# A two-layer decoder on one core: layer 1's cross-attention on row halves and column quarters, as a pipeline of single tiles that starts inside the self-attention

## The chip, the cores and the metric

The kernel runs on one core of a Trainium2 chip. The metric is device time in microseconds (us) of one execution. Three runs of the kernel before gave a median of 2326.64 us (2325.31 to 2329.75).

The engines are named as the profile names them: PE (TensorE, matrix multiplies and transposes; PEld is its weight load), DVE (VectorE), ACT (ScalarE), POOL (GpSimd), SP (SyncE, which here only issues DMAs). "PSUM" is the memory that PE writes and that DVE and ACT can read; "SBUF" is the working memory that all engines read.

## The reference: what is computed

Two batches of 1024 tokens with 256 features (2048 tokens in all), and a context of 64 rows for each batch. Two post-norm layers, each of a self-attention, a cross-attention to the context and a feed-forward net, with a layer norm after each of the six. The part that the change rewrites is the fifth of the six, layer 1's cross-attention with 16 heads of 16 features:

```
qh = (x   @ wq.T) split into 16 heads of 16
kh = (ctx @ wk.T) split likewise            # 64 context rows
vh = (ctx @ wv.T) split likewise
z  = qh kh^T / 4                            # per head: 1024 x 64 per batch
z  = where(mask, -1e10, z)                  # mask[b, token, context row]
z  = softmax(z, over the 64 context rows)
z  = (z vh) put back to 256 features
x  = layernorm(x + z @ wo.T)
```

It is followed by a feed-forward net whose inputs are quantised with one scale for the whole tensor: the largest absolute value over all 2048 tokens has to be known before the first matrix product of that net can start. So there is a hard joint between the cross-attention and what follows.

## The kernel before

Tokens are held in 4 groups of 512 (`NG`, `GT`), a group in 4 tiles of 128 tokens (16 tiles, `NT`). The weights and biases of layer 1 are prepared in `prepare`, a generator that the expert feed-forward net of layer 0 (`l0_ffn`) advances by one `yield` per step of its own loop, from step 4 of 32 on, so that this work lies beside the matrix products of that net.

**PSUM and pools.** `bank()` gives one of 3 PSUM banks of 128x512 f32, `wide()` one of 2 pairs of banks (128x1024), `acc()` a single bank of its own. `evac` copies PSUM to SBUF, on DVE and ACT in turn unless `by` names one. `weight` gives one of 5 SBUF buffers.

**What sets the order.** Inside `tc.manual_schedule(engines=...)` the named engines run their instructions in the order in which the Python code issues them; engines that are not named are ordered by the framework's scheduler. Every engine runs its own queue strictly in order; waits between engines are semaphores that the framework puts in.

**Layer 1's self-attention** (`l1_attn`, L1205) is a loop over 128 units, written out by hand for PE, DVE and ACT. A unit does the products of one block of keys (`products`, L1322: 8 matrix products on row halves into two `wide` buffers, then two exponentials of 128x1024 on ACT), the mixing of the block before (`mix`, L1355: 4 products on column quarters into `acc`), and two `maxima` (L1270: 4 products into `bank`s and 4 reductions on DVE) for a step that comes 9 units later. So the last 9 units (119 to 127) have no `maxima`. Everything else is hung onto unit numbers with `at(unit, f, ...)`: projections, stacking DMAs, and for each group of 512 tokens the transposes (`turned`), the residual on POOL, the output product (`output`), the layer norm (`normed`) and the transposed copy of the normed group (`onward`). For group 2 these fall in units 122 to 128; for group 3 they are left for the next stage as `self.ends`.

**Layer 1's cross-attention** (`l1_xattn`, L1647) orders only PE by hand; DVE, ACT and POOL are the scheduler's. It first builds `kblk`, keys laid out as a block diagonal: for each chunk `m` of 8 heads a matrix of 128 rows (8 heads of 16 features) by 512 columns (8 heads of 64 context rows), zero outside a head's own block. Then for each of 16 tiles:

- `queries` (once per group, L1666): 4 products of 128x512.
- `softmax` (L1677): POOL fills a tile with -1e10, PE makes the scores in two products over all 128 rows and 512 columns, DVE copies the unmasked ones over the fill (L1690), DVE takes the maximum per head (L1695), POOL subtracts it (L1696), ACT exponentiates (L1697).
- `turn` (L1700): 8 transposes on PE; ACT copies one half out, DVE the other.
- `mix` (L1716): 8 products with the transposed weights as the stationary side and 34 columns (two heads, each 16 values and a column of ones that gives the sum); DVE takes the reciprocal and scales (L1727, L1729).
- `back` (L1734): 2 transposes; `output` (L1745): 2 products of 256 columns, the residual on DVE, and the layer norm (`normalise`, L165, and `scaled`, L214) for one to three tiles at a time, on DVE. The running maximum for the quantisation goes to `xm`, 9 columns.

PE's program goes through n = 0..18 with `softmax(n + 2)`, `turn(n)`, `output(n - 3)`, `back(n - 2)`, `mix(n - 1)`.

## Time and profile before

| what | value |
|---|---|
| median of three runs | 2326.64 us |
| the profiled execution: its own time | 2326.49 us |
| its span (first to last instruction) | 2324.7 us |
| busy share of the span: PE, PEld, DVE, ACT, POOL | 97%, 67%, 71%, 48%, 39% |
| unit 119 of layer 1's self-attention starts (end of the last `maxima`) | 2093.3 us |
| last mixing product of the self-attention ends | 2122.7 us |
| first scores of the cross-attention start | 2128.4 us |
| last column of `xm` is ready | 2243.0 us |
| rest of the quantised net | to 2324.7 us |
| PE busy from 2122.7 to 2243.0 us | 110.6 of 120.3 us |

The profile's times are counted from the start of the span. A group of instructions is named by its line, its engine and its operation, then output <- inputs by the program's names, with partitions x elements; after it stand the count, the busy time and the mean time of one. PE's records need care: an f32 product shows as two records, and matrix products overlap, so the distance from one start to the next says more than the duration of one.

### The profile page before, as it was taken

To read this page: it belongs to the slowest core of one execution; us is meant where nothing else is said; L and a number is where in the kernel's file an instruction comes from. 1 tells how busy PE (TensorE), PEld (TensorE's weight loads), DVE (VectorE), ACT (ScalarE), POOL (GpSimd) and SP (SyncE) were. 2 spreads that over 40 slices of the span, in tenths; PEclk is the share of its full clock that TensorE was granted. 3 is DMA by queue.
4 is the path that set the end of the run, shared out by engine and by line. 5 is a ranking of instruction groups with operands and counts; after the bars stand their busy time and mean duration, and the time that the engine had idled before them with its cause. 6 is when DMAs were issued, how large, how long until landed. Compare 5 with 4: busy or idle time off the path is not lost.

```text
span 2324.7 us, 37116 instructions
## 1 busy us (share of the span) xinstructions
PE 2253.7 (97%) x13964; PEld 1558.2 (67%) x13969; DVE 1650.6 (71%) x2836; ACT 1117.5 (48%) x1754; POOL 916.0 (39%) x791
## 2 busy tenths in 40 slices
PE   8999999999999999999999999999999999999986
PEld 3555545555546788999999999999744454554752
DVE  5888788998787356555556555456789687994778
ACT  4666566566564322333233333333157565665355
POOL 4676576677566444324334333333211101102420
PEclk9999999999999999999999999999999999999998
DMA  6777678577686120101001011000313121310001
GB/s 155 175 174 170 147 180 185 133 182 176 143 196 165 41 62 1 37 15 31 19 32 37 19 31 37 15 1 1 62 17 51 25 45 28 52 22 1 1 1 37
DMA packets 103831, 168.68 MB, mean 73 GB/s; under 512 B 47602, under 2 KB 65508, under 8 KB 103652
## 3 DMA queue, kind: packets, MB, share of 16 engines
q1 hardware_dynamic: 96804, 147.94, 27.9%
q10 hardware_dynamic: 6848, 18.36, 3.3%
q8 instruction: 111, 1.82, 0.3%
q14 instruction: 68, 0.56, 0.1%
HBM read 34.10 MB, written 2.10 MB: 16 GB/s over the span
## 4 chain that ended last, share of the span: by engine, by line
PE 87%; DVE 6%; ACT 3%; issue 2%; DMA 1%; SPq 1%; POOL 0%; ACTq 0%; DVEq 0%; POOLq 0%
PE unit L1025 17%; PE acc L1073 10%; PE wide L325 10%; PE acc L410 9%; PE bank L1073 7%; PE acc L1362 5%; PE bank L280 4%; PE bank L1285 4%; PE bank L428 2%; PE bank L744 2%; PE wide L1331 2%; PE wide L1338 2%; PE bank L304 2%; DVE most L1295 1%; PE bank L1194 1%
## 5 line engine op out<-in xcount | busy, mean ns | idle before, releaser
L340 DVE TENSOR_REDUCE nm<-wide 128x1 f32<-128x1024 f32 x256 | 300.7, 1214 | 58.2 <-PE wide L325 57.1
L1348 ACT ACTIVATE w<-wide 128x1024 f32<-128x1024 f32 x256 | 248.2, 1021 | 128.4 <-PE wide L1338 127.5
L1295 DVE TENSOR_REDUCE most<-bank 128x1 f32<-128x512 f32 x476 | 295.4, 681 | 16.1 <-PE bank L1285 15.5
L325 PE MATMUL wide<-k,q 64*128 64x512 f32 x1024 | 264.3, 624 | 9.3 <-ACT p L345 7.6
L356 POOL TENSOR_SCALAR p<-p,sums 128x1024 f32<-128x1024 f32 x128 | 143.4, 1121 | 249.2 <-DVE sums L353 249.2
L410 PE MATMUL acc<-turned,v 128*64 128x256 f32 x2048 | 235.1, 382 | 0.2 <-issue 0.2
L410 PEld LDWEIGHTS acc<-turned,v 128*64 128x64 f32 x2048 | 141.8, 137 | 111.5 <-issue 35.0
L1014 ACT ACTIVATE mhT<-mhT,cols 128x256 f32<-128x256 f32 (+1 forms) x256 | 143.4, 607 | 146.5 <-DVE mhT L1042 103.4
L345 ACT ACTIVATE p<-wide,nm 128x1024 f32<-128x1024 f32 x128 | 142.8, 1115 | 125.0 <-DVE nm L340 104.6
L923 POOL TENSOR_TENSOR hs<-hs,mhT 128x1024 f32<-128x1024 f32 x31 | 102.4, 3304 | 237.5 <-DVE hs L921 220.2
L1025 PE MATMUL unit<-xT,w 128*128 128x256 f32 x768 | 182.2, 379 | 0.0
L370 DVE STREAM_TRANSPOSE blocks<-p 128x1024 f32<-128x1024 f32 x128 | 158.0, 1234 | 25.3 <-DMA turned<-blocks 9.2
L1082 DVE SCALAR_TENSOR_TENSOR r<-acc,gates,r 128x128 f32<-128x128 f32 x256 | 77.7, 345 | 138.1 <-PE acc L1073 138.1
L325 PEld LDWEIGHTS wide<-k,q 64*128 64x128 f32 x1024 | 89.8, 186 | 126.2 <-issue 78.1
L370 DVE STREAM_TRANSPOSE blocks<-r 128x1024 f32<-128x1024 f32 x128 | 153.8, 1202 | 0.0
L1025 PEld LDWEIGHTS unit<-xT,w 128*128 128x128 f32 x768 | 140.9, 190 | 17.0 <-issue 0.5
L356 POOL TENSOR_SCALAR r<-r,sums 128x1024 f32<-128x1024 f32 x128 | 143.8, 1124 | 0.0
L345 ACT ACTIVATE r<-wide,nm 128x1024 f32<-128x1024 f32 x128 | 142.1, 1111 | 0.0
L1285 PE MATMUL bank<-kst,qst 64*128 64x512 f32 x476 | 133.1, 471 | 9.2 <-DVE most L1295 8.0
L1362 PE MATMUL acc<-w,v 128*32 128x512 f32 x1024 | 137.6, 606 | 1.1 <-ACT w L1348 1.1
L1285 PEld LDWEIGHTS bank<-kst,qst 64*128 64x128 f32 x476 | 66.8, 185 | 107.0 <-DVE most L1295 80.9
L393 POOL COPY turned<-blocks 32x1024 f32<-32x1024 f32 x128 | 131.9, 1031 | 4.0 <-DVE blocks L370 0.3
(351 smaller groups left out, 4373.7 us busy)
## 6 DMA issues: line engine op xcount, KB each, us to landing
turned<-blocks SPq DMA_DIRECT2D x636, 128.0 KB, 2.4
turned<-blocks ACTq DMA_DIRECT2D x132, 128.0 KB, 2.5
w<-in_L_ffn_W SPq DMA_DIRECT2D x16, 1024.0 KB, 5.5
q<-q SPq DMA_DIRECT2D x64, 128.0 KB, 2.4
k<-k SPq DMA_DIRECT2D x32, 128.0 KB, 2.3
qst<-qh SPq DMA_DIRECT2D x48, 64.0 KB
qst<-ql SPq DMA_DIRECT2D x48, 64.0 KB, 2.3
kst<-kh SPq DMA_DIRECT2D x48, 64.0 KB, 2.3
```

The lines of the kernel that those rows point to most:

```text
L325: nc.tensor.matmul(sc[h][:, kb, :], lhsT=q[rows, qi, at : at + P], rhs=k[rows, ki, :], start=True, stop=True,)
L340: nc.vector.tensor_reduce(nm, sc, AX.XY, ALU.max, negate=True)
L345: nc.scalar.activation(p, sc.rearrange("p a c -> p (a c)"), AF.Exp, bias=nm, accum_out=sums[:, 0, h : h + 1],)
L356: nc.gpsimd.tensor_scalar(p, p, sums[:, 1, h : h + 1], 1.0, ALU.mult, ALU.mult)
L370: nc.vector.transpose(blocks[m][:, :, :, h, qt, :], p.rearrange("p (k r q) -> p r k q", r=4, q=32))
L410: nc.tensor.matmul(av[own[h], 0:256].rearrange("p (t i q) -> p i t q", t=2, i=4), lhsT=vals[u][:, kt, own[h]], rhs=p[:, h], start=kt == 0, ...
L1025: nc.tensor.matmul(v[:, m, :], lhsT=up[e][k][:, f : f + P], rhs=self.halves[g][k], start=k in (1, 2, 5) and m == 0, stop=True, skip_group_ ...
L1073: nc.tensor.matmul(ps[at][:, m * P : (m + 1) * P], lhsT=h[k][:, c, m * P : (m + 1) * P], rhs=down[e][k][:, c, :], start=k in (1, 2, 5) and ...
L1285: nc.tensor.matmul(sc[a], lhsT=stack[b, jp, "q"][rows, q0 : q0 + P], rhs=stack[b, jp, "k"][rows, kb * 512 : (kb + 1) * 512], start=True, s ...
L1295: nc.vector.tensor_reduce(most[n][:, kb, qt, h : h + 1], sc[a], AX.X, ALU.max, negate=True)
L1348: nc.scalar.activation(slot[:, k, :], ps[k].rearrange("p a q -> p (a q)"), AF.Exp, scale=0.25)
L1362: nc.tensor.matmul(mixed[n][o : o + 32, :], lhsT=vals[b][:, kt, 17 * h : 17 * h + 32], rhs=pT[:, a, :], start=kt == 0, stop=kt == 7, tile_ ...
```

## The change

Eight things are done.

1. **Scores on row halves.** The 128 rows of a chunk are split into two halves of 64 rows (4 heads each); each half needs only the 256 columns of its own heads. Instead of 2 products of 128 rows x 512 columns there are 4 of 64 rows x 256 columns, two at a time on the two halves of the array.
2. **The mask as a product.** `prepare` transposes the mask (`masked`, bf16) and builds `never` (-1e30 on a diagonal, bf16). Two bf16 products on row halves put the mask into PSUM first; the scores are added to it. The fill on POOL, `keep` and the predicated copy go. In `prepare` this adds four steps, each one DVE copy, four bf16 transposes and one copy out of PSUM, and four `yield`s, so all that follows in the generator comes four steps later.
3. **Sums and division before the mixing.** The column of ones goes. DVE sums the exponentials (`weights`), takes the reciprocal, and POOL multiplies the tile by it. So a tile now has two POOL passes of 128x1024 (subtract, multiply) and, for the last two tiles, each pass is split between POOL and DVE.
4. **Mixing on column quarters.** The values become the stationary side (32 columns), two transposed tiles the moving side (256 columns): 8 products per two tiles. The result is already transposed, so `back` goes.
5. **Who copies.** ACT copies the raw scores out (`copied`), and both halves of the transposed tile, the mixed result and the layer norm's scaling are ACT's; DVE keeps the maximum (now read from PSUM), the sum, the residual and the statistics.
6. **One tile per step, all engines by hand.** The loop over u = 4..21 orders PE, DVE, ACT and POOL.
7. **Four tiles inside the self-attention.** `keys` (the block-diagonal keys, now on POOL) at unit 84, the queries of group 0 at units 118 and 119, the scores and copies of tiles 0 to 3 at units 120, 122, 124, 126, their exponentials and divisions at 123, 125, 127 and in the next stage. These copies go through two `bank`s each and are on DVE.
8. **POOL by hand in the self-attention.** POOL joins the engines that run in program order there.

The layer norm works on two tiles at a time, and `xm` has 8 columns. The diff, cut to its core:

```diff
@@ l1_attn
+            self.l1_cross()
+            x = self.cross
+            at(last - 44, x["keys"])
+            for m in range(2):
+                at(last - 10 + m, x["queries"], 0, m)
+            for n in range(4):
+                for f in ("scores", "copied"):
+                    at(last - 8 + 2 * n, x[f], n)
+                for f in ("exponentials", "weights") if n < 3 else ():
+                    at(last - 5 + 2 * n, x[f], n)
...
-            engines = {mybir.EngineType.PE, mybir.EngineType.DVE, mybir.EngineType.Activation}
+            engines = {
+                mybir.EngineType.PE, mybir.EngineType.DVE, mybir.EngineType.Activation,
+                mybir.EngineType.Pool,
+            }
@@ prepare
-        nc.vector.tensor_scalar(self.keep, mask, 0.0, None, ALU.is_equal)
...
+        for n in range(0, T // P, 4):
+            both = tmp.tile([P, 4, 2, SK], BF16, tag="both", name="both")
+            nc.vector.tensor_copy(both, mask[:, n : n + 4, :].unsqueeze(2).to_broadcast([P, 4, 2, SK]))
+            ps = self.ps_t.tile([P, 1024], BF16, tag="t", name="bankb")
+            for i in range(4):
+                nc.tensor.transpose(
+                    ps[:, i * P : (i + 1) * P], both[:, i].rearrange("p a k -> p (a k)"), self.identb
+                )
+            self.evac(self.masked[:, n * P : (n + 4) * P], ps[:, 0 : 4 * P])
+            yield
@@ new: l1_cross
+        def queries(g, m):
...
+            self.evac(qT[g][:, m, :], ps, 0.25, by=nc.scalar if m and g else nc.vector)
+        def scores(n):
...
+            if n < 4:
+                ps = [self.bank() for _ in range(2)]
+            else:
+                both = self.wide()
+                ps = [both[:, a, :] for a in range(2)]
+            raw[n] = ps if n < 4 else both
+            for r, a in zip(rows, range(2)):
+                nc.tensor.matmul(
+                    ps[a], lhsT=self.masked[r, n * P : (n + 1) * P],
+                    rhs=self.never[r].rearrange("p h k -> p (h k)"), start=True, stop=True,
+                    skip_group_check=True,
+                )
+            for m in range(2):
+                for r, a in zip(rows, range(2)):
+                    nc.tensor.matmul(
+                        ps[a][:, m * 256 : (m + 1) * 256], lhsT=qT[g][r, m, i * P : (i + 1) * P],
+                        rhs=self.kblk[r, g // 2, m, 4 * a : 4 * a + 4, :].rearrange("p h k -> p (h k)"),
+                        start=False, stop=True, skip_group_check=True,
+                    )
+        def scaled(n, by, op):
+            p = prob[n]
+            halves = [(nc.gpsimd, 0, H)]
+            if n >= NT - 2:
+                halves = [(nc.gpsimd, 0, H // 2), (nc.vector, H // 2, H)]
...
+        def copied(n):
...
+            if n < 4:
+                for a in range(2):
+                    nc.vector.tensor_copy(
+                        p[:, 8 * a : 8 * a + 8, :].rearrange("p h k -> p (h k)"), ps[a]
+                    )
+                nc.vector.tensor_reduce(nm, p, AX.X, ALU.max, negate=True)
+            else:
+                src = ps.rearrange("p a (h k) -> p (a h) k", k=SK)
+                nc.scalar.copy(p, src)
+                nc.vector.tensor_reduce(nm, src, AX.X, ALU.max, negate=True)
+            scaled(n, nm, ALU.add)
+        def exponentials(n):
+            if n < NT:
+                nc.scalar.activation(prob[n], prob[n], AF.Exp)
+        def weights(n):
...
+            nc.vector.tensor_reduce(z, prob[n], AX.X, ALU.add)
...
+            nc.vector.reciprocal(rz, z)
+            scaled(n, rz, ALU.mult)
@@ l1_xattn
+            def mix(r):
...
+                ps = self.acc().rearrange("p (c q) -> p c q", c=2)
                 for c in range(2):
+                    for q in range(4):
+                        o = slice(32 * q, 32 * q + 32)
+                        nc.tensor.matmul(
+                            ps[o, c, :], lhsT=self.vblk[:, r // 4, 4 * c + q].rearrange("p a i -> p (a i)"),
+                            rhs=turned[r][:, 4 * (q // 2) + 2 * c + q % 2, :], start=True, stop=True,
+                            tile_position=(0, 32 * q),
+                        )
...
+                self.evac(mixed[r], ps, by=nc.scalar)
             def output(n):
...
                 nc.vector.tensor_tensor(res[g][:, i, :], ps, self.x[g][:, i, :], ALU.add)
+                if k:
+                    moments[r] = self.moments(res[g], range(i - 1, i + 1))
+            def normed(r):
...
+                by = nc.vector if r == NT // 2 - 1 else nc.scalar
+                self.scaled(new[g], res[g], range(i, i + 2), *moments.pop(r), by)
...
+                for m in range(2):
+                    x["queries"](1, m)
+                turn(0)
+                for u in range(4, NT + 6):
+                    turn(u - 3)
+                    x["scores"](u)
+                    x["exponentials"](u - 1)
+                    x["copied"](u)
+                    x["weights"](u - 1)
+                    output(u - 5)
+                    if u % 2:
+                        normed((u - 7) // 2)
+                        x["queries"]((u + 4) // 4, u // 2 % 2)
+                    else:
+                        mix((u - 4) // 2)
+                    if u < 8:
+                        self.ends[u - 4]()
```

## The prediction

> **What bounds the kernel now.** I read the page first, then busy time by stretch, the cross-attention's groups, the chain of waits, and the order in time. On the page PE is busy 97% of the span; by stretch this holds from the end of the last `maxima` (2093.3 us) to the last column of `xm` (2243.0).
>
> ```profile
> core 0: us, PE busy (x) PEld busy (x) DVE busy (x) ACT busy (x) POOL busy (x), PEclk, DMA share, GB/s
> 2093.30:2122.70 29.40, 27.96 (x189) 12.09 (x186) 8.61 (x22) 20.54 (x25) 5.22 (x8) 1.00 0.01 2
> 2122.70:2243.00 120.30, 110.58 (x620) 80.41 (x620) 88.72 (x183) 39.25 (x61) 48.94 (x42) 0.99 0.00 1
> ```
>
> In the self-attention's tail (first row) DVE and POOL are mostly free, ACT is not. In the cross-attention PE binds: tile 1's `turn` starts at 2145.74, tile 14's at 2223.94, so a tile takes 6.0 us. The groups, kept apart by shape:
>
> ```profile
> L1686 PE MATMUL wide<-w,lxqT 128*128 128x512 f32 x64 | 30.9, 606 | 0.0
> L1696 POOL TENSOR_TENSOR lxp<-lxp,lxnm 128x1024 f32<-128x1024 f32 x16 | 30.4, 1902 | 34.0 <-DVE lxnm L1695 34.0
> L1722 PE MATMUL acc<-vblk,lxpT 128*128 128x34 f32 x256 | 29.9, 273 | 0.0
> L1695 DVE TENSOR_REDUCE lxnm<-lxp 128x16 f32<-128x1024 f32 x16 | 19.3, 1209 | 0.0
> L1697 ACT ACTIVATE lxp<-lxp 128x1024 f32<-128x1024 f32 x16 | 16.9, 1058 | 21.8 <-POOL lxp L1696 21.8
> ```
>
> POOL, DVE and ACT wait here for each other (34.0, 21.8) under PE's cover. The chain of waits shows the same three once, where PE does not cover them, before the first tile (start, us, what):
>
> ```profile
> 2130.52 1.31 DVE lxp L1690
> 2131.86 1.23 DVE lxnm L1695
> 2133.16 1.91 POOL lxp L1696
> 2135.09 1.06 ACT lxp L1697
> ```
>
> A hop between engines costs 0.02 to 0.08. The end of the tail in time: ACT's layer norm of group 2 stands ahead of the last exponentials, and PE waits 1.14 for them.
>
> ```profile
> 2117.69 2.07 ACT L224 ACTIVATE xg<-r,off,rstd 128x256 f32<-128x256 f32 x4
> 2119.66 1.92 ACT L1348 ACTIVATE w<-wide 128x1024 f32<-128x1024 f32 x2
> 2120.72 1.96 PE L1362 MATMUL acc<-w,v 128*32 128x512 f32 x8 [1.14 <-ACT w L1348]
> ```
>
> **The change part by part.** *PE.* A tile costs 6.2 now: scores 1.72 (L1686), `turn` 0.87, mixing 1.71 (L1722), `back` 0.22, output 0.86, queries 0.86. Scores on f32 row halves have a row in layer 0 (L325, 8 records of 512 columns in 1.92): 8 records of 256 take 0.96; the mask pair 0.23 (a pair in L1331); together 1.2. Column quarters (L1362) take 1.0 per 8 records of 512; two tiles' mixing has 16 of 256, 1.0, so 0.5 a tile. New sum: 1.2 + 0.87 + 0.5 + 0.86 + 0.86 = 4.3.
>
> *The loop.* PE's 4.3 doesn't set the pace; the order does. In the built program the maximum's only wait is ACT's copy of the same tile. Copying 1024 columns from PSUM I price as L1348, 1.02; the maximum from PSUM as L1290, 1.21. With u's copy ending at 0, in an even unit: maximum to 1.24, POOL's subtraction (1.90) 1.32 to 3.22, exponential to 4.31, next copy to 5.23 (back-to-back instructions overlap by about 0.1 on ACT, 0.07 on DVE). In an odd unit the layer norm of two tiles sits on ACT between copy and exponential, and its offset stands on DVE behind maximum 1.24, sum 2.38, reciprocal 2.60, residual 2.95, offset 3.04. ACT then scales twice (0.59, 0.49) to 4.15, copies two halves to 5.11, exponentiates to 6.07, copies to 6.99. Two units take 12.2, so 6.1 a tile: PE's 6.0 again, now on a chain over ACT, DVE and POOL. The queries' ACT copy adds 0.5 in unit 11. Units 8 to 14: 37.1; 14 to 15, with the subtraction split, 5.0.
>
> *The tail.* Unit 121's mixing ends at 2103.8 now. Add 3.5 (two query units of 1.75), 0.5 (tile 0's scores, 1.2, less 0.7 of a wait they fill), 1.2 (tile 1's): 2109.0, called s. Unit 122's transposes end at s+1.4 (one bank is awaited), unit 123 at 5.4, 124 at 10.9, 125 at 13.0, unit 126's mixing at 15.2, tile 3's scores at 16.4. DVE copies (1.3) and reduces (1.21) them before it reaches group 2's offset, s+19.1; ACT, which waits for it with the last exponentials behind, scales to 21.2 and exponentiates to 23.0; the last mixing ends at s+23.6 = 2132.6, against 2122.7 now: +9.9. Bounds: +6.5 (8.3 of added PE work less the 1.8 of waits) and +14 (DVE's sums queued ahead as well); I keep the walk's value. The keys (4 POOL passes at unit 84, at most 1.27 each, L922) hide in POOL's 0.58 of 20 us.
>
> *Filling.* Transposed group 1.1, wait for `raw` 0.65, quotient 0.55, queries 3.45, two `turn`s 1.8, scores 1.2, 0.25 of waits, then 1.3 on ACT: the first loop copy (unit 4) ends at 2142.9. Units 4 to 8 also carry group 3's end. Unit 4 takes the even 5.2. In unit 5 PE has queries (1.75) and two output products (3.45) ahead of the next transposes and scores, and POOL a residual of 2.38 (L1410) ahead of its subtraction: 7.9. In unit 6 DVE reaches group 3's offset 4.5 after the copy; ACT then scales four times (2.07), copies two halves (0.96), exponentiates (0.96) and copies (0.92): 9.4. Unit 7 has offset 3.04, scaling 1.1, queries 0.5, a transposed copy 0.5, halves, exponential and copy 2.84: 8.0. In all 30.5; between 24 (four units at 6.1) and 35 (if unit 5's two delays add up).
>
> *Draining.* After unit 15's copy: DVE is 0.6 late with the maximum, split passes collide on two SBUF inputs (L923, below: about 1.6 instead of 0.95, four times), the last exponential ends at 9.3 behind an offset (6.3), two scalings and two copies; then sum 10.6, reciprocal 10.8, split product 12.4. DVE's half of the last copy comes after the statistics of tiles 10 and 11 and the maximum of the pair before: 17.2. Mixing 1.0, copy 0.6, output 0.5, then DVE still has an offset and a maximum before it (22.1); residual 0.4, statistics 1.3, power 0.8, scaling 0.9, maximum 0.7, with 0.3 of hops: 26.5 (20 without this queueing, 30 if every half collides in full).
>
> Sum: 2142.9 + 30.5 + 37.1 + 5.0 + 26.5 = 2242.0, against 2243.0: -1.0. To it come three small terms. PE is idle 3.6 us at the end of the tail; the trace has a gap like it:
>
> ```profile
> 1694.28 0.66 PE L1316 MATMUL bank<-ident,cz 128*128 128x128 f32 x4 [3.27 <-POOL cz L1309]
> 1690.00:1695.00 5.00, 1.59 (x10) 1.00 0.57 93
> 1695.00:1700.00 5.00, 4.61 (x20) 0.54 0.01 3
> 1700.00:1705.00 5.00, 5.00 (x36) 0.78 0.00 0
> ```
>
> (the last three: granted clock third from the right). After 3.27 idle it fell to 0.54 and 0.78, some 3.4 us of PE time; I take +1.5 (0 to 3.4), as PE waits for ACT in part of it. The Trainium skill (TensorE: Matmul & The Clock Gate, Part 1) says that one idle window of about 3.4 us halves the clock and a busy one restores it; by it alone this term would be 1.7. `prepare`: 16 bf16 transposes at 0.09 (L1605, 36 in 3.0) beside a PE that is full, and the steps that move towards the end: +2 (0 to 4; its DVE copies, at most 0.7 each, hide under PE, with DVE busy 13.8 of 20 us there, and cost that much each if they don't; SP's loads of these weights move with them, behind two loads of experts' weights; PE waits for no load of this stage in the trace). POOL in program order in the self-attention: +1 (0 to 2: at worst something waits once for the 2.0 memset at L1236). Together +4.5, less the 1.0: +3.5. The profiled execution took 2326.5 (0.15 under the median), so 2330.
>
> The skill's rule that speaks against the change: tiling speeds up TensorE but not the emptying of PSUM, which may become the bottleneck (TensorEngine Tiling (Array Packing), PSUM Bottleneck). By it, counting ACT's copies, exponential and layer norm as throughput, 4.1 a tile, PE would still bind and the time be 2305; the chain above, from this trace's rows, is slower than either throughput.
>
> **The rivals.**
> *The shared SBUF side* (slower). Two-input DVE passes of layer 0 stretch POOL's:
>
> ```profile
> L923 POOL TENSOR_TENSOR hs<-hs,mhT x31: 2351/3333/3398, 871.8 to 1622.7; 128x1024 f32<-128x1024 f32 x31
> L1696 POOL TENSOR_TENSOR lxp<-lxp,lxnm x16: 1900/1902/1905, 2133.2 to 2223.6; 128x1024 f32<-128x1024 f32 x16
> ```
>
> (minimum/median/maximum ns.) If the sums, which now run beside POOL, do this too, 1.90 becomes 2.85: +0.95 in each of 11 units, 2340. Against it: 16 passes at L1696 kept within 5 ns beside DVE's one-input work. It decides from 2.3 a pass on.
> *The layer norm doesn't delay ACT* (faster): if offsets are ready when ACT's copy ends, scaling fits in POOL's 1.9 and units 6, 7, 9, 11, 13, 15 save 3.4, 3.0, 1.8, 2.2, 1.8, 1 (their lengths less the even 5.2, as far as the offset alone makes them): 2317. Against it: DVE's built order.
> *PE stays the bound* (faster): 4.4 a tile, 11 units in 48 instead of 72.6: 2305. For it only PE's present 97%.
> *Halves don't run side by side* (the change doesn't do what it says): scores cost 2.0, +4 in tail and filling, 2334. Against it: L325.
>
> **How the numbers follow.** What a measurement here can tell from no change is about 0.2%, 4.7 us. The walk holds with 0.55 (2323 to 2337: 0.36 within 0.2%, 0.18 above, 0.01 below); SBUF side 0.15; no delay 0.15; PE bound 0.07; halves 0.08 (0.06 slower, 0.02 the same). So faster 0.23, same 0.38, slower 0.39. The range 2315 to 2343 leaves out 2305 and the rest of the tails.
>
> **What would show it.** Right: the last mixing of the self-attention near 2133, copies from PSUM at alternating distances of about 5.2 and 7.0, ACT's layer norm waiting for DVE, POOL at 1.9, the drain 25 or more. Wrong: equal distances below 5.5 (PE or no delay), POOL over 2.3, a tail that grows by less than 6, or a granted clock under 0.9 through the loop.

## The result, and the profile after

The changed kernel takes 2339.89 us (median of four executions, 2338.3 to 2342.1) against 2325.97 of the kernel before beside it (2322.45 to 2329.75): a ratio of 1.006, 95% interval 1.0042 to 1.0078. On a second occasion, at the end of the experiments, the same two took 2341.19 and 2330.95: 1.004 (1.0025 to 1.0055). So it is slower by about half a per cent, more than the 0.2% that can be told from no change. Predicted were 2330 and a range of 2315 to 2343, with 0.38 for "within 0.2%" and 0.39 for "slower": the time lies in the range, some 10 us above the point. As a change, +3.5 us were predicted and 13.9 came.

The profiled execution after took 2339.48 us, its span 2337.7, so 13.0 longer than before's 2324.7. To find where, I cut both spans at seven events that both traces have, and took the differences of their times:

| stage, from the event of the row above to | before, us | after, us | difference | predicted |
|---|---|---|---|---|
| the first `unit` matmul on the experts (L1025 on `xT`, `w`) | 836.3 | 836.3 | 0 | 0 |
| the last such matmul starts | 799.9 | 805.8 | +5.9 | +2 |
| DVE's first early maximum starts | 31.3 | 34.1 | +2.8 | 0 |
| its last early maximum starts | 24.8 | 24.8 | 0 | 0 |
| the last maximum starts (end of the self-attention's steady part) | 400.7 | 401.8 | +1.1 | +1 |
| the last self-attention mixing ends (the tail) | 29.8 | 40.8 | +11.0 | +9.9 |
| the last column of `xm` starts (cross-attention) | 119.9 | 110.7 | -9.2 | -10.9, +1.5 for the clock |
| the end of the span | 82.1 | 83.4 | +1.3 | 0 |

(Each is rounded to 0.1; unrounded, the rows add to 13.0.) The trade that the prediction is mostly about, a longer tail for a shorter cross-attention, came out at +1.8 where +0.5 was predicted. The time was lost ahead of it: 8.7 us before the first maximum of layer 1, in a part of the kernel that the change hardly seems to touch.

Busy time by stretch after; these are the tail and the cross-attention, the two stretches that the prediction showed of before:

```profile
core 0: us, PE busy (x) PEld busy (x) DVE busy (x) ACT busy (x) POOL busy (x), PEclk, DMA share, GB/s
2103.50:2143.60 40.10, 36.12 (x233) 16.65 (x232) 21.05 (x36) 23.20 (x27) 15.32 (x11) 0.98 0.00 1
2143.60:2255.00 111.40, 83.32 (x508) 52.95 (x508) 71.80 (x140) 57.96 (x90) 56.56 (x40) 0.88 0.00 1
```

PE was busy for 110.6 of 120.3 us in the cross-attention, now for 83.3 of 111.4: it no longer binds. No other engine does either; DVE, the next, has 64%. What binds is an order of short waits. The groups, by shape, of tail and cross-attention (busy us, mean ns of one, then the idle time ahead of them):

```profile
L1767 DVE TENSOR_REDUCE lxnm<-wide 128x16 f32<-128x1024 f32 x12 | 14.7, 1224 | 23.8 <-ACT lxp L1766 9.1 <-ACT kh L1766 6.3 <-ACT ql L1766 4.9
L1731 PE MATMUL wide<-v,lxqT 64*128 64x256 f32 x96 | 13.8, 407 | 3.2 <-ACT lxqT L76 3.2
L1825 PE MATMUL acc<-lxpT,vblk 128*32 128x256 f32 x128 | 11.3, 428 | 3.4 <-DVE lxqT L72 1.8 <-ACT lxpT L74 1.3 <-DVE lxpT L70 0.2
L1743 POOL TENSOR_TENSOR lxp<-lxp,lxnm 128x1024 f32<-128x1024 f32 x4 | 7.6, 1903 | 13.8 <-DVE lxnm L1767 13.8
L1724 PE MATMUL wide<-never,masked 64*128 64x512 bf16 x24 | 4.9, 405 | 0.0
```

Row halves and column quarters do what they say: the scores of twelve tiles (L1731) take 13.8 us and the mixing of all sixteen (L1825) 11.3, where before each took some 30 for sixteen. POOL's pass keeps its 1.90. DVE's maximum waits for ACT's copy of the same tile, POOL for the maximum. The chain of waits shows one odd unit and one even unit whole (start, us, what):

```profile
2203.91 0.91 ACT lxp L1766
2204.84 1.23 DVE lxnm L1767
2206.07 1.14 DVE lxz L1778
2207.23 0.25 DVE lxrz L1780
2207.48 0.28 DVE r L1846
2207.76 0.38 DVE off L219
2208.17 1.09 ACT xg L224 x2
2209.26 0.48 ACT lxqT L76
2209.74 0.96 ACT lxpT L74 x2
2210.70 0.96 ACT lxp L1772
2211.66 0.91 ACT qh L1766
2212.59 1.24 DVE lxnm L1767
2213.96 1.91 POOL qh L1743
2215.89 1.06 ACT qh L1772
2216.95 0.91 ACT ql L1766
```

The lower four steps are the even unit that was predicted (maximum, subtraction, exponential, copy), the upper ones the odd unit, with the offset `off` as the fifth thing that DVE does after ACT's copy. Where the 8.7 us arise is shown by two other views. In the experts' stretch, PE's waits after and before:

```profile
PE bankb L1560 <- DVE both L1557: 4.1, 4, 1.0
```

```profile
PE bank L1572 <- DVE twice L1566: 1.1, 1, 1.1
```

(us in all, times, longest). L1560 are the four transposing steps that the change puts into `prepare`. In order of time, the first of them:

```profile
989.70 0.61 DVE L1082 SCALAR_TENSOR_TENSOR r<-acc,gates,r 128x128 f32<-128x128 f32 x2 [0.48 <-PE acc L1073]
990.22 0.41 DVE L1557 CAST both<-mask 128x512 bf16<-128x512 uint8 x1
990.69 0.40 PE L1560 MATMUL bankb<-identb,both 128*128 128x128 bf16 x4 [1.03 <-DVE both L1557]
```

The cast needs nothing of this moment (the mask was loaded long before), but it stands in DVE's queue behind an expert's sum, which itself waits for the matmuls just done. PE, whose next work are the transposes, stands still for the sum and the cast, 1.04 us, four times over. And ahead of the first maximum, the order of time at PE and at the queues that load the stacks:

```profile
1668.68 2.05 PE L1073 MATMUL acc<-w2s,mhT 128*128 128x128 f32 x16 [0.70 <-DVE r L1082]
1670.57 1.95 PE L1073 MATMUL bank<-w,hs 128*128 128x128 f32 x16
1670.76 0.51 SPq L1263 DMA_DIRECT2D qst<-xg  x1
1670.77 0.52 ACTq L1263 DMA_DIRECT2D qst<-xg  x1
...
1675.22 1.17 PE L1287 MATMUL wide<-kst,qst 64*128 64x512 f32 x4 [2.70 <-DMA qst<-xT]
```

The first stacks of the queries leave at 1670.76, as a matmul of the last expert ends, and PE then waits 2.70 us for them. SP's queue waited for this matmul:

```profile
SPq L1263 <- PE acc L1073: 5.4, 1, 5.4
```

The same wait in the kernel before:

```profile
SPq L1261 <- DVE r L1082: 6.3, 2, 5.9
```

There it was a DVE result that the queue waited for (5.9 us at the longest), and the first of these loads left 10.1 us after the first projection (L1194) began, not 18.7. A load that waits for a matmul which has nothing to do with its data waits for memory. In the built programs, the tiles of `qst` lay at bytes 142816 to 159200 of a partition before; the change opens the pools `qk` and `lxq` ahead of `la1` and `st`, so that they now lie at 181984 to 198368, over the experts' `mhT` (171104 to 187488) and `hs` (192608 to 204896), which the last experts' matmuls read to the end. (Before, the two upper ones of the four tiles lay over the other buffer of `mhT`, but the tile that is filled first did not.)

### The profile page after: what moved, and what is told of

Its sections match the earlier page's. It is cut to its first block, busy times and chain, and to the rows that moved or that the text cites. A ratio compares the mean times of both kernels' runs of the same rounds, so it can differ in the third digit from the quotient of the medians.

```text
span 2337.7 us, 36999 instructions
## 1 busy us (share of the span) xinstructions
PE 2239.8 (96%) x13916; PEld 1538.6 (66%) x13921; DVE 1648.3 (71%) x2813; ACT 1140.2 (49%) x1787; POOL 932.7 (40%) x792
## 4 chain that ended last, share of the span: by engine, by line
PE 82%; DVE 8%; ACT 4%; DMA 2%; SPq 2%; issue 2%; POOL 0%; ACTq 0%; DVEq 0%; POOLq 0%
PE unit L1025 16%; PE acc L1073 10%; PE wide L325 8%; PE acc L410 8%; PE bank L1073 7%; PE acc L1364 5%; PE bank L1287 4%; PE bank L280 4%; PE bank L428 2%; PE bank L744 2%; PE wide L1333 2%; PE wide L1340 2%; PE bank L304 2%; SPq L389 1%; DMA turned<-blocks 1%
## 5 line engine op out<-in xcount | busy, mean ns | idle before, releaser
L325 PE MATMUL wide<-k,q 64*128 64x512 f32 x1024 | 264.7, 625 | 10.3 <-ACT p L345 8.0
L1025 PE MATMUL unit<-xT,w 128*128 128x256 f32 x768 | 182.2, 379 | 0.0
L370 DVE STREAM_TRANSPOSE blocks<-p 128x1024 f32<-128x1024 f32 x128 | 158.0, 1234 | 26.9 <-DMA turned<-blocks 9.6
L1025 PEld LDWEIGHTS unit<-xT,w 128*128 128x128 f32 x768 | 140.9, 190 | 17.0 <-issue 0.5
```

The costliest lines, as they stand in the source:

```text
L325: nc.tensor.matmul(sc[h][:, kb, :], lhsT=q[rows, qi, at : at + P], rhs=k[rows, ki, :], start=True, stop=True,)
L370: nc.vector.transpose(blocks[m][:, :, :, h, qt, :], p.rearrange("p (k r q) -> p r k q", r=4, q=32))
L1025: nc.tensor.matmul(v[:, m, :], lhsT=up[e][k][:, f : f + P], rhs=self.halves[g][k], start=k in (1, 2, 5) and m == 0, stop=True, skip_group_ ...
```

## The experiments

Each is judged by the stage that it changes, in its own profile, and by its time beside the kernel before. The part ahead of the first expert matmul, which none of the edits touches, took 834.5 to 840.0 us in the thirteen profiles, so only differences of events are compared.

### The mask's part alone

The kernel before, with the four steps added to `prepare` (into a tile that nothing reads):

```diff
+        masked = late.tile([P, T], BF16, name="masked")
         yield
+        for n in range(0, T // P, 4):
+            both = tmp.tile([P, 4, 2, SK], BF16, tag="both", name="both")
+            nc.vector.tensor_copy(both, mask[:, n : n + 4, :].unsqueeze(2).to_broadcast([P, 4, 2, SK]))
+            ...
+            yield
```

> The kernel before, with the mask's four steps in `prepare` alone (a cast, four bf16 transposes and a copy each, into a tile that nothing reads). Theory: this part costs what the stretch of the experts grew by, 5.9 us (4 x 1.04 of wait, 1.6 of transposes and what the later steps' move adds), and nothing later: about 2332 against 2326. The prediction's term, +2 (0 to 4), would give 2328. Rival: the 5.9 come from elsewhere in the change (other places in SBUF, the removed `keep`); then this stays within 2 us of before.

Measured: 2332.68 against 2328.94 us, 1.0016 (1.0005 to 1.0026). The experts' stretch took 805.8 us, as in the kernel after, against 799.9; from there to the first maximum 31.3, as before. So the 5.9 belong to this part and the 2.8 do not. In the medians it is 3.7 us, with an interval of 1.2 to 6.1 that holds both +2 and 5.9; the stage, which repeats to 0.1 in every kernel with these steps, tells them apart.

### The casts a step ahead

```diff
+        both = cast(0)
         yield
         for n in range(0, T // P, 4):
-            both = tmp.tile([P, 4, 2, SK], BF16, tag="both", name="both")
-            nc.vector.tensor_copy(both, mask[:, n : n + 4, :].unsqueeze(2).to_broadcast([P, 4, 2, SK]))
             ps = self.ps_t.tile([P, 1024], BF16, tag="t", name="bankb")
             ...
             self.evac(self.masked[:, n * P : (n + 4) * P], ps[:, 0 : 4 * P])
+            both = cast(n + 4)
             yield
```

> The kernel after, with one thing moved: in `prepare`, each of the four DVE casts of the mask (`both`) is issued one step earlier than the four PE transposes that read it, instead of right before them. Theory: of the 5.9 us that the stretch of the experts (to the last `unit` matmul) is longer after than before, 4 x 1.04 us are PE standing still for a cast that DVE, in program order, reaches only after an expert's sum (0.61) and then does in 0.42; the other 1.6 are the 16 transposes. Expected: the last `unit` matmul starts 4.2 us earlier (at about 1645.9, not 1650.0), PE waits for no cast, and the whole takes 4 us less than after, about 2336. Rival: the added steps cost by moving later ones (the weights' loads, the gates), and then the last `unit` matmul stays within 1 us of 1650.0.

Measured: 2334.86 against 2328.94, 1.0028 (1.0018 to 1.0037). The experts' stretch fell from 805.8 to 801.0, and PE waits for no cast. The expected absolute start (1645.9) is to be read with the start of the stretch, which was 1.4 later in this execution; by it, 4.8 were gained where 4.2 were expected. What is left is +1.1 to before: four steps of 0.40, less the one wait of this kind that before had (1.1, shown above), and some 0.6 more. So the wait was the main cause (4.1 of the 5.9 by the waits, 4.8 by the stretch), and the move of the later steps cost at most that rest. The rival fell.

### The held pools in their old places

```diff
-            qkp = self.l1qkp = self.hold.enter_context(self.pool("qk", 1))
-            self.lxq = self.hold.enter_context(self.pool("lxq", 1))
+            qkp = self.l1qkp = self.hold.enter_context(self.pool("qk", 1, side="right"))
+            self.lxq = self.hold.enter_context(self.pool("lxq", 1, side="right"))
```

> The kernel after, with one thing undone: the pools `qk` and `lxq` that are held until the cross-attention are opened from the other end of SBUF, so that `la1` and `st` lie again where they lay before the change (the stacks from byte 126688 on, away from the experts' `mhT` and `hs`). Theory: the first `maxima` (L1287) waits 2.7 us for the stacks of the queries because their tiles now lie over what the last experts' matmuls (L1073) read, and their loads are held back until 1670.8. Expected: the loads of the queries' stacks start some 10 us after the first projection (L1194), not 18.7; PE's wait of 2.7 before the first `maxima` is gone; the time falls by 2.7, to about 2337. Rival: POOL's order by hand holds the loads back (the memsets of `v` come earlier in it); then the wait stays at 2.7 and the time within 1 us of after.

Measured: 2336.8 against 2328.94, 1.0033 (1.0023 to 1.0042). The queue's waits of this kernel, same view as above:

```profile
SPq L1263 <- DVE r L1082: 5.3, 1, 5.3
```

The loads wait for the DVE result again, as before the change. The first stack of the queries left 10.1 us after the first projection, PE's wait of 2.70 is gone, and the stage took 32.1 (34.1 after, 31.3 before). POOL's order, still by hand, did not hold the loads back. 2.0 came of the 2.7 expected: in place of the long wait stand two short ones for DVE's maxima (1.0 together, 0.4 in the kernel before).

### POOL left to the scheduler

```diff
-            engines = {
-                mybir.EngineType.PE, mybir.EngineType.DVE, mybir.EngineType.Activation,
-                mybir.EngineType.Pool,
-            }
+            engines = {mybir.EngineType.PE, mybir.EngineType.DVE, mybir.EngineType.Activation}
```

> The kernel after, with one line undone: POOL is left to the scheduler in layer 1's self-attention. The prediction gave its order by hand +1 us (0 to 2). From the first early maximum's last (1692.2 before, 1701.0 after) to the last maximum the stretch took 400.7 before and 401.8 after; the kernel with the mask's steps alone, POOL scheduled, took 401.6. If the order by hand costs, this stretch falls to 400.7 here; if the 1.1 is no more than the spread between executions, it stays at 401.5 to 402.5.

Measured, one execution of 2345.13 us: the stretch took 402.2 us. So the order by hand costs nothing that this one execution shows. All twelve profiles other than that of the kernel before have 401.6 to 402.5, also the one with the mask's part alone, whose self-attention is untouched, and there is one profile of before. Whether its 400.7 is a lucky execution or something common to the twelve stays open; it is 1 us.

### The first four tiles behind the self-attention

```diff
-            for m in range(2):
-                at(last - 10 + m, x["queries"], 0, m)
-            for n in range(4):
-                for f in ("scores", "copied"):
-                    at(last - 8 + 2 * n, x[f], n)
-                ...
@@ l1_xattn
                 for m in range(2):
+                    x["queries"](0, m)
+                for u in range(4):
+                    x["scores"](u)
+                    if u:
+                        x["exponentials"](u - 1)
+                    x["copied"](u)
+                    if u:
+                        x["weights"](u - 1)
+                for m in range(2):
                     x["queries"](1, m)
```

> The kernel after, without one part of the change: the first four tiles' queries, scores, maxima and exponentials are issued behind the self-attention, ahead of the loop, in the same form. It tells what this part is worth by itself. From the rows of after: the tail loses its 11 us (the last mixing ends as in the kernel before, 29.8 after the last maximum instead of 40.8), and the first copy of the loop comes some 25 after it instead of 10.7 (queries 3.6, scores, copy, maximum, POOL, exponential of tile 0 some 8, then four tiles at some 4 us), so the whole is 3 us slower than after (0 to 6). If the pipeline ahead of the loop is paced by the chain over DVE, POOL and ACT as in the even units (5.3 a tile), it is 6 slower; if the tail's growth was mere PE work that is now hidden elsewhere, it is faster than after.

Measured: 2344.25 against 2328.91, 1.0067 (1.0053 to 1.0081). The tail took 29.8, before's length to 0.1, so its 11.0 us of growth are these four tiles' and nothing else's. The first loop copy started 26.3 after the last mixing, not 9.7, and the cross-attention took 127.4 instead of 110.7. Net, the early tiles are worth 5.7 us: the 6 of the expectation's second case, not its central 3.

### Group 2's layer norm ahead of tile 3's copy

```diff
+            extra[last - 2].insert(0, (normed, (2,)))
             ...
                     for k, f in ((10, turned), (10, residual), (14, normed), (16, onward)):
-                        at(first + k, f, g)
+                        if f is not normed or g < 2:
+                            at(first + k, f, g)
```

> The kernel after, with one order changed in the self-attention's tail: group 2's layer norm is issued ahead of tile 3's copy and maximum (in the same unit, 126), so that DVE computes its offset before 1.29 and 1.22 us of tile 3's work. Theory: PE's last wait of the tail (3.79 us for ACT's exponentials, behind the layer norm, behind the offset at 2137.56) goes back to the offset's place on DVE; the offset comes at 2134.6, 2.9 earlier, the wait falls below 1.5 us, PE's clock isn't halved (the last mixing took 2.79 for 8 matmuls that take 1.07 at full clock), and the tail is 4 us shorter in all (3 to 5). Rival: PE's own added work (8.3 us) sets the tail, and the time moves less than 1.

Measured: 2336.94 against 2328.91, 1.0034 (1.0021 to 1.0047); the tail took 37.0 instead of 40.8, so -3.8. The end of the tail after, in time, then that of this kernel:

```profile
2137.56 0.15 DVE L219 SCALAR_TENSOR_TENSOR off<-mv,rstd 128x4 f32<-128x4 f32 x1
2137.74 2.07 ACT L224 ACTIVATE xg<-r,off,rstd 128x256 f32<-128x256 f32 x4 [2.87 <-DVE off L219]
2139.72 1.91 ACT L1350 ACTIVATE w<-wide 128x1024 f32<-128x1024 f32 x2
2140.78 2.79 PE L1364 MATMUL acc<-w,v 128*32 128x512 f32 x8 [3.79 <-ACT w L1350]
```

```profile
2140.21 0.10 DVE L219 SCALAR_TENSOR_TENSOR off<-mv,rstd 128x4 f32<-128x4 f32 x1
2140.45 2.08 ACT L224 ACTIVATE xg<-r,off,rstd 128x256 f32<-128x256 f32 x4
2140.81 1.29 DVE L1762 COPY kl<-bank 128x512 f32<-128x512 f32 x2 [0.50 <-PE bank L1733]
...
2143.49 1.97 PE L1364 MATMUL acc<-w,v 128*32 128x512 f32 x8 [0.80 <-ACT w L1350]
```

Offset, then copy, not the other way round, and PE waits 0.80 instead of 3.79. The clock answers: in the kernel after, the two slices of 3 us behind the wait of 3.79 were granted 0.63 and 0.80 (third number from the right; the columns are those of the first view above), 1.7 us of PE time lost:

```profile
2141.00:2144.00 3.00, 3.00 (x11) 0.65 (x8) 1.35 (x2) 1.58 (x2) 0.00 (x0) 0.63 0.00 0
2144.00:2147.00 3.00, 2.61 (x13) 1.95 (x13) 1.30 (x4) 1.07 (x2) 1.90 (x1) 0.80 0.00 0
```

After the wait of 0.80 every slice had 1.00. (The expectation put the whole 2.79 of the last eight matmuls down to the clock. Part of it is the wait for the second of the two exponentials: with the clock at 1.00 they still took 1.97.) The cross-attention took 111.7 in this run, 1.0 more than after; no run says why.

### The offset first in the odd units

```diff
                     x["copied"](u)
+                    if u % 2:
+                        offset((u - 7) // 2)
                     x["weights"](u - 1)
```

(`offset` is the one instruction of `scaled` that computes `off`; `normed` then only scales.)

> The kernel after, with one instruction moved: in the loop's odd units DVE computes the layer norm's offset right behind the maximum (it is ready: POOL's power ends before), not behind sum, reciprocal and residual. Theory (the chain over ACT sets the pace, and ACT waits 3.35 us for the offset in every odd unit): the scaling starts 1.7 earlier, so odd units shrink from 7.25 to about 5.6 in units 9, 11, 13 and from 10 in unit 7 by as much, and the drain by some 2; together 8 us less than after (6 to 10), about 2332. Rival: something else paces the odd units (PE's queries and output products, or POOL's two passes); then the distances between the copies of odd and even units stay within 0.5 us of 7.25 and the time within 2 us of after.

Measured: 2330.02 against 2328.94, 1.0008 (0.9998 to 1.0018): this one instruction's place takes back most of the loss. The cross-attention took 100.8 instead of 110.7, -9.9. ACT's layer norm in an odd unit of the kernel after:

```profile
2195.61 1.09 ACT L224 ACTIVATE xg<-r,off,rstd 128x256 f32<-128x256 f32 x2 [3.35 <-DVE off L219]
```

ACT with the edit:

```profile
2199.41 0.99 ACT L1766 COPY lxp<-wide 128x1024 f32<-128x1024 f32 x1
2201.77 1.09 ACT L1871 ACTIVATE xg<-r,off,rstd 128x256 f32<-128x256 f32 x2 [1.36 <-DVE off L1856]
...
2205.14 1.01 ACT L1766 COPY qh<-wide 128x1024 f32<-128x1024 f32 x1
...
2209.49 1.06 ACT L1772 ACTIVATE qh<-qh 128x1024 f32<-128x1024 f32 x1 [1.63 <-POOL qh L1743]
2210.45 0.99 ACT L1766 COPY ql<-wide 128x1024 f32<-128x1024 f32 x1
```

ACT waits 1.36 for the offset where it waited 3.35, and the wait lies beside POOL's subtraction, which ACT needs anyway. The copies of units 8 to 15 stand 5.4, 5.3, 5.3, 5.7, 5.3, 5.3, 4.9 apart; in the kernel after they stood 5.3, 7.25, 5.3, 7.7, 5.3, 7.25, 4.9 apart. Odd units became even units, a little more than expected (5.6).

### All moves together

The kernel after with the four moves above that gained, and group 3's offset likewise ahead of the sums in unit 6:

```diff
                     x["copied"](u)
+                    if u % 2:
+                        offset((u - 7) // 2)
+                    if u == 6:
+                        self.offset3()
                     x["weights"](u - 1)
```

> The kernel after with five moves together, none of which changes what is computed: the mask's casts a step ahead; the held pools from the other end of SBUF; the offset first in the loop's odd units; group 3's offset likewise in unit 6; group 2's layer norm ahead of tile 3's copy in the tail. If the causes are separate and add up: 4.8 less in the experts' stretch, 2.0 before the first maximum, 4 in the tail, 9.9 in the loop, 3.6 in unit 6 (its offset at 2170.96 could stand at 2167.1, with ACT idle 3.87 for it), 24 in all from first expert matmul to the end, so 2315 or a little more where before takes 2326: a ratio of 0.995 (0.992 to 0.998). If another limit (PE, or POOL's two passes of 1.9 in each 5.3) stands close behind, at most half of the last two come, and the ratio is 0.998 or above.

Measured: 2313.93 against 2328.91, 0.9936 (0.9924 to 0.9949). From the first expert matmul to the end it took 1475.3 us; after took 1501.4, before 1488.4. The 26.1 are 4.8 in the experts' stretch, 2.0 ahead of the first maximum, 3.8 in the tail and 15.4 in the cross-attention, less 0.6 in the self-attention, and 0.6 at the end. The first three and 9.9 of the fourth are what the four moves gave one by one, so these causes are separate. The other 5.5 came with group 3's offset, which was not tried alone, and with the moves meeting: unit 6 shrank from 10.2 to 6.2, unit 7 by 1.0 more than with the odd units' offsets alone, and the first copy came 0.5 earlier behind the tail.

### The copy ahead of the exponential

Now the units from 8 on take 5.3, whether odd or even (5.7 with a copy of queries): copy, maximum, subtraction, exponential, next copy. The last link is no data, only ACT's order.

```diff
-                    x["exponentials"](u - 1)
                     x["copied"](u)
+                    x["exponentials"](u - 1)
```

> The kernel of the five moves together, and one more: in each unit of the loop ACT copies tile u from PSUM ahead of the exponential of tile u-1, not behind it. Theory: the 5.3 us that every unit takes there is the chain copy, maximum 1.24, POOL's subtraction 1.90, exponential 1.06, next copy, closed into a loop only by ACT's order (no data goes from the exponential to the next copy); with the copy first the chain spans two units, and the next limits are PE (28 to 29 us busy in the 32.2 of six units, 4.8 a tile), POOL (3.8 a tile and 0.7 for a power in every second) and ACT (some 4.1). Expected: distances between copies of 4.5 to 5.0 where they were 5.3, some 0.5 less in ten or eleven units, 5 us less in all (2 to 8): 2309. Rival: PE is the bound already (90% busy) and the distances stay within 0.1 of 5.3.

Measured: 2307.08 against 2327.53, 0.991 (0.9895 to 0.9924). The cross-attention took 89.9 instead of 95.3. The copies of units 8 to 15 stand 4.3, 5.1, 4.3, 5.6, 4.2, 5.2, 4.2 apart, 4.7 on average. In order of time, PE (one tile without queries, the next with):

```profile
2167.92 1.09 PE L1827 MATMUL bank<-ident,qh 128*128 128x128 f32 x8
2168.94 0.39 PE L1744 MATMUL wide<-never,masked 64*128 64x512 bf16 x2
2169.17 1.03 PE L1751 MATMUL wide<-v,lxqT 64*128 64x256 f32 x8
2170.13 1.13 PE L1862 MATMUL bank<-lxwoT,lxo 128*128 128x256 f32 x4
2171.09 1.88 PE L1726 MATMUL acc<-xT,lxwqT 128*128 128x512 f32 x4
2172.81 1.04 PE L1827 MATMUL bank<-ident,ql 128*128 128x128 f32 x8
```

No wait is left in these rows. The stretch around them, in the columns of the first view above:

```profile
2165.00:2195.00 30.00, 27.89 (x201) 17.87 (x198) 25.98 (x46) 23.69 (x36) 23.91 (x16) 1.00 0.00 1
```

PE is busy for 27.9 of 30.0 us, DVE for 26.0, and four waits of PE are left in the loop, 2.1 us together. So PE comes closest to binding again, now at 4.7 a tile instead of 6.0.

The same edit on the kernel after, offsets where they were:

> The kernel after with the last move alone: in each unit of the loop ACT copies tile u ahead of the exponential of tile u-1; the offsets stay where they were. If ACT's order closes the chain, an even unit falls from 5.3 to PE's 4.3, and an odd one, where ACT still waits for the offset (copy, 3.35 of wait less nothing, scaling 1.0, copies 1.0, next copy at 6.4), from 7.25 to about 6.4: a pair takes 10.7 instead of 12.5, 9 us less in all (5 to 12), 2331. If the odd unit's wait is what counts and even units recover nothing, 4 us less or fewer.

Measured: 2336.28 against 2330.95, 1.0026 (1.0014 to 1.0039); the cross-attention 106.5 instead of 110.7. From copy 8 to 10, 10 to 12 and 12 to 14 it took 11.4, 11.8 and 11.4 us where after took 12.6, 13.0 and 12.6: 1.2 a pair, not 1.8, and three pairs, not five. Units 4 to 8 hardly moved (32.3 for 32.7; ACT waits 3.63 and 2.40 there for offsets); the last copy came 1.4 closer to the one before, and the drain behind it took 1.5 longer. So -4.2 of the 9. Behind the offsets' move the same edit gave 5.4: most of its gain does not depend on that move, but it gives less while ACT also stands in front of offsets.

The kernel after, timed once more:

> The kernel after, unchanged, on the same chip and beside the same runs of before as the last experiment. By its stages it should stand 13 us above before (a ratio of 1.0056). The single moves, timed on other occasions, stood at 1.0028 to 1.0034, which is 2 to 4 us less than their stages say if after is at 1.0060; if after stands at 1.005 or less here, that gap is the spread between occasions, and the stages are right.

Measured: 2341.19 against 2330.95, 1.004 (1.0025 to 1.0055). That is under the 1.005 of the expectation, which then puts the gap between the single moves' ratios and their stages down to the occasion; but the intervals of the two occasions overlap, so this is likely and not shown. By stage, the experts' stretch, the tail and the cross-attention repeat to 0.1. The others do not: 34.5 for 34.1 to the first maximum, 26.7 for 24.8 in the early maxima (four of the thirteen profiles have 26.3 to 26.9 there, whatever the edit), 402.4 for 401.8 in the self-attention, 82.2 for 83.4 at the end. So the table's +1.3 at the end is scatter, and of its +1.1 in the self-attention 0.7 is what this kernel differs from itself.

## Why the prediction was right, and where it was wrong

**The bounds, the tail.** Right in mechanism and nearly in size. From the end of tile 1's scores (s = 2118.68 after) the offset came at s+18.9 (predicted 19.1), ACT had scaled at s+21.1 (21.2) and exponentiated at s+22.9 (23.0). The last mixing ended at s+24.9 instead of s+23.6: from the last exponential on it took 1.9 where 0.6 was predicted, 0.8 of it the clock (the same step took 1.1 at full clock in the run with the tail's order changed). The clock's term held: 1.7 us of PE time lost in all after 3.79 idle (predicted 1.5, 0 to 3.4). The Trainium skill's rule (TensorE: Matmul & The Clock Gate, Part 1: an idle window of about 3.4 us halves the clock) gives 1.7 as well, as an estimate; for the gap of 3.27 that the prediction shows, where some 3.4 were lost, it gives half of what was measured.

**The filling.** The first loop copy ended 10.7 after the last mixing (10.3). Units 4 to 8 took 5.3, 7.3, 10.2, 9.9, together 32.7 (5.2, 7.9, 9.4, 8.0, together 30.5): unit 7 was under-sized. ACT's scaling, the queries' copy and the copy of `xT` stand there behind the late offset, PE's transposes and scores wait for them, and ACT in turn twice waits 0.72 for PE.

**The loop.** "The order does" is shown. Copies stood alternately 5.3 and 7.25 apart (5.2 and 7.0), 7.7 with queries (7.5); units 8 to 14 took 38.2 (37.1). The edit of one instruction's place made all of them 5.3 to 5.7, the edit of ACT's order 4.7 on average: none of this changes any engine's work.

**The draining.** 25.0 from copy 15's end to the last column (26.5). The split passes took what the prediction expected of a collision, POOL's half 1.48 (1.6) and not 0.95, half of a whole pass.

**`prepare`.** Wrong, and the largest miss: +2 (0 to 4) was 5.9. The step that failed is "its DVE copies, at most 0.7 each, hide under PE, with DVE busy 13.8 of 20 us there". Each cast took only 0.42, and there was room on DVE: the 13.8 are those of 1640 to 1660 us, and from 985 to 1075, where the four steps came to lie, DVE was busy for 48.8 of 90 us before. But a share of idle time says nothing of where in the queue the instruction stands: behind a sum that waits for PE, right in front of PE's next work. The price of lost cover, 0.7 a step at most, was also too low, as it counted the cast and not what it queues behind: 1.04 a step.

**Places in memory.** Not in the prediction at all: +2.8, of which the experiment gave back 2.0. The diff shows the cause in plain sight, the pools' order. "PE waits for no load of this stage in the trace" was true of the kernel before.

**POOL by hand.** +1 (0 to 2) was nothing, by the one execution without it. That the stage grew by 1.1 makes the term look right, and this is luck: the growth has no cause that these runs show.

**The rivals.** *The shared SBUF side* fell on its own terms: POOL's whole passes stayed at 1.90, far from 2.3, with DVE's sums beside them. *The layer norm doesn't delay ACT* was not what the change does, but it is what the offset's place makes it: -9.9 for the odd units alone and -15.4 with all five moves against the 13 that it was priced at. *PE stays the bound* needs one more order, and then comes to 4.7 a tile with some waits of PE left, 2307.08 against the 2305 that it was priced at for 4.4 and without most of the losses outside. The Trainium skill's rule on tiling (TensorEngine Tiling (Array Packing), PSUM Bottleneck), that the emptying of PSUM may become the bottleneck, is not what the runs show: in the kernel after no engine's throughput binds, and in the fastest kernel PE (27.9 of 30.0 us) is closer to it than DVE (26.0) and ACT (23.7), which empty PSUM. *Halves* run side by side, at the predicted prices: in the rows of the fastest kernel the mask's pair starts at 2168.94, the scores 0.23 later (0.23), and the next product 0.96 after these (0.96).

**What was to show it.** Distances, layer norm, POOL and tail came as listed under "right"; the drain (25.0) on its line. A granted clock below 0.9 "through the loop" was listed under "wrong": the filling had 0.86 (2153 to 2189), the loop itself 0.96 (2189 to 2228), so this sign did not come. What the 0.86 cost the filling, where ACT twice waits for PE, no run shows.

**The sum.** Tail and cross-attention came to +1.8 for +0.5, `prepare` to +5.9 for +2, memory to +2.8 for 0, the self-attention to +1.1 for +1, the end to +1.3 for 0 (this profile has 83.4 there, the twelve others 82.0 to 83.0). The chances gave 0.55 to the walk with a range of its own up to 2337; the measured 2339.89 lies outside this, by the two terms that lie nowhere near the cross-attention. The full range up to 2343 takes in the rival of the shared SBUF side, priced at 2340, which fell; 0.21 of the 0.39 for "slower" stood on it and on the halves. So the walk through tail and cross-attention was right on its merits, and that the whole time still lies in the range is partly luck.

## What to carry to other kernels

An engine that is idle for almost half of the time (DVE in these steps) hides nothing if the new instruction stands in its queue behind one that waits: write down what is in front of it and who waits behind, and issue whatever is ready early a step earlier. When a loop is bound by no engine, list the links of its chain, and look for those that are only an engine's program order; moving the layer norm's offsets, instructions of 0.15 us, and swapping two others took the cross-attention from 110.7 to 89.9 us here without changing any work. When a diff opens memory pools in another order, compare what each tile now lies over and when that is released; the sign in a trace is a load that waits for an unrelated matmul.

## What the runs showed that was not expected

The kernel after, with the six moves, beats both: 2307.08 us, 0.991 of before. So the change was less a bad trade than an unfinished one.

Executions of a program vary in ways that a span does not tell apart from an edit: the untouched first part took 834.5 to 840.0 us, and 18 early maxima of layer 1 took either 24.8 or 26.3 to 26.9, in nine and four of the thirteen profiles, the kernel after among both. Spans alone would have given the casts' move 2.8 us instead of 4.8 and the tail's move a loss of 1.9 instead of a gain of 3.8.
